# Six seams of a decoder layer, put in another order

## The chip, the cores and the metric

The program runs on one core of a Trainium2 chip. The metric is the device time of one execution in microseconds (us); lower is better. PE is the matrix engine (PEld its weight loads), DVE the vector engine, ACT the scalar engine, POOL the GpSimd engine, and SP the queue that issues DMAs here. Each engine works through its own instructions in the order in which the program lists them and waits for others by semaphores, so the order of the listing is the schedule.

## The reference, cut to what matters

```python
x = x + attn(layernorm(x))                  # 8 x 112 tokens, 512 wide, 16 heads of 32, rotary, causal
ln = layernorm(layernorm(x)) * ln_w + ln_b
q, k, v = lin(fp8(ln / q_in)), lin(fp8(ln / k_in)), lin(fp8(ln / v_in))    # 16 / 8 / 8 heads of 128
qx = lin(fp8(ln / qx_in)); kx, vx = ctx @ w_kv_x                           # ctx: 8 x 375 x 512
core, xout = gqa(norm(q), norm(k), v), gqa(norm(qx), norm(kx), vx)
x = x + fp8(concat(core, xout) / smooth) @ wproj * scale
h = silu(g) * u                              # (g, u) = layernorm(x) @ ternary(w_gate_up)
x = x + rms_norm(h) @ ternary(w_proj)        # hidden width 2048
```
`fp8` clips to 448 and rounds to a float8 and back. The result has 8 x 112 rows of 512 numbers.

## The kernel before

The whole layer is one straight program; nothing is looped on the chip. Its stages, with the lines of the listing:

The first attention takes the 8 batches in two halves of four. It loads x tiles `xb` (L94), `vec` (all small vectors, L99) and weights; DVE works out constants from `vec` (L117 to L145: inverse scales `rins`, `lnw`, `lnb`, `rsm`, `psc`, `epsc`, `hln`); `norm_stats` and `norm_apply` make the normed rows `h`, PE transposes them (L375), and `project_qk` (L388) makes queries and keys with the rotary turn on DVE and POOL. Per batch, `batch(b, last)` (L535) lists: `values(b)`, `attended(b-2)`, `scores(b)` (L438), `turned(b-1)` (transposes of the weights, L471, and their copy `pt`), and `softmaxed` (DVE adds the mask, L451, and reduces, L458; POOL subtracts, L459; ACT takes the exponential, L462). `joined` adds the output to `xb` and norms the sum again; `to_tiles` (L533) copies the sums by DMA from tiles of 112 rows to tiles `xs` of 128.

The rounding to float8 of the second norm's output is cut into 32 tiles: 2 halves x 4 column chunks k x 4 scale sets m (query, key, value, context query). `qgroups` lists groups that share one transposed input: PE transposes it once into a PSUM buffer (`quantise_turn`, L297), and `quantise_begin` (L304) lets ACT make `y` (scale and bias, L315) and `big` (L227). At a group's last tile it also has the next group transposed ahead. `quantise(n, begin)` (L318) lists n steps: a begin (if asked), for an earlier tile the two clips on DVE (L231, L232) and the sum `f8t` on POOL (L234), and for a still earlier one the subtraction into `xq[m]` on DVE (L333). Calls stand in the last two projections, in the batches, and after the first units. PSUM has four buffers `ps` and four `pa`, each handed out in turn.

Weights of the second attention come through `load_raw` from a queue; `split_chunk(s, what, k)` (L258) splits one chunk into a high and a low part on ACT and DVE or POOL and then lists the next load on SP. The second attention then runs as 64 units: 32 `Own` (4 sets s of heads x 8 batches b) and 32 `Context` units. A unit's `project` lists its projections and, between them, later stages of earlier units through `advance(stage, g)`:

```python
            advance("score", g)
            advance("turn_p", g)
            advance("out", g)
            self.pkv = pa()
```
`score` is q times k (L739); `weigh` takes exponentials (L753), the reciprocal `ri` (L638) and the product on POOL (L640); `turn_p` transposes it (L762); `out` is the output projection of five units earlier (`project_out`, L597 with `cq`). `own_background` lists weight splits at the end of each own unit. At unit 32 the pools of the own units close, and the first weights `wx` and context tile `ct` of the context units are loaded (`load_wx`, `load_ct`); `keys(j)` (L801) multiplies them.

The feed-forward makes `hid` in blocks of 256 with the sums of squares `sq` (POOL, L1067); `down(c, hid, last)` (L1177) projects down. In the last call it first sums `sq` over partitions by PE (L1182), takes the root on POOL, and then per tile of 128 rows adds the product to `ys`, scales by `rstd`, adds `xs` and stores.

Of the kernel before, what the change touches and what calls it, by code (L numbers as in the profile page):

```python
# [11 lines left out]
F32 = mybir.dt.float32  # L12
# [7 lines left out]
P = 128  # L20
# [18 lines left out]
def decoder_layer(  # L39
# [73 lines left out]
    nc.gpsimd.memset(gones[64:128, 64:128], 1.0 / 128.0)  # L113

    rins = const.tile([P, 16], F32, tag="rins", name="rins")  # L117
    nc.vector.reciprocal(rins, vec[:, V_INS : V_INS + 16])
    lnw = const.tile([P, 16], F32, tag="lnw", name="lnw")
    lnb = const.tile([P, 16], F32, tag="lnb", name="lnb")  # L120
    for m in range(4):
        cut = slice(4 * m, 4 * m + 4)
        nc.vector.tensor_mul(lnw[:, cut], rins[:, cut], vec[:, V_LNW : V_LNW + 4])
        nc.vector.tensor_mul(lnb[:, cut], rins[:, cut], vec[:, V_LNB : V_LNB + 4])
    rsm = const.tile([P, 32], F32, tag="rsm", name="rsm")
    nc.vector.reciprocal(rsm, vec[:, V_SM : V_SM + 32])
    nc.vector.tensor_scalar_mul(rsm[:, 0:16], rsm[:, 0:16], vec[:, V_SC + 2 : V_SC + 3])
    psc = const.tile([P, 1], F32, tag="psc", name="psc")
    nc.vector.tensor_mul(psc, vec[:, V_SC + 5 : V_SC + 6], vec[:, V_SC + 4 : V_SC + 5])

    epsc = const.tile([P, 4], F32, tag="epsc", name="epsc")
    nc.vector.tensor_mul(epsc, vec[:, V_SC : V_SC + 4], vec[:, V_SC : V_SC + 4])
    nc.vector.reciprocal(epsc, epsc)
    nc.vector.tensor_scalar_mul(epsc, epsc, LN_EPS)
    sgn = const.tile([P, 4], F32, tag="sgn", name="sgn")
    nc.vector.tensor_scalar(sgn, vec[:, V_SC : V_SC + 4], 0.0, 2.0, ALU.is_ge, ALU.mult)
    nc.vector.tensor_scalar_add(sgn, sgn, -1.0)

    hln = const.tile([P, 8], F32, tag="hln", name="hln")
    for i, (sg, f) in enumerate(((0, ISD), (None, ISD), (1, 1.0), (None, 1.0), (3, ISD), (None, ISD), (None, 1.0), (None, 1.0))):  # L140
        v = vec[:, V_HLN + i : V_HLN + i + 1]
        if sg is None:
            nc.vector.tensor_scalar_mul(hln[:, i : i + 1], v, f)
        else:
            nc.vector.tensor_scalar(hln[:, i : i + 1], v, sgn[:, sg : sg + 1], f, ALU.mult, ALU.mult)  # L145


    def col(i):
        return vec[:, i : i + 1]
# [154 lines left out]
    def quantise_begin(t):  # L304
        i, half, k, m = qtiles[t]
        if m == qgroups[i][2][0]:
            if ("tp", i) not in qstate:
                quantise_turn(i)
            qstate["ln"] = qstate.pop(("tp", i))[:, :SH]
        if m == qgroups[i][2][-1] and i + 1 < len(qgroups) and qgroups[i + 1][0] == half:  # L310
            quantise_turn(i + 1)
        y = s0.tile([P, SH], BF, tag="y", name=uid("y"), bufs=4)

        at = slice(4 * m + k, 4 * m + k + 1)
        nc.scalar.activation(y, qstate["ln"], AF.Identity, bias=lnb[:, at], scale=lnw[:, at])  # L315
        qstate["y", t] = round_begin(y, s0, 6)

    def quantise(n, begin=True):  # L318


        for _ in range(n):
            if begin:
                quantise_begin(qstate["begun"])
                qstate["begun"] += 1
# [12 lines left out]

    with ExitStack() as st:
# [166 lines left out]
        for b in range(HB):  # L505
            ln_apply(b)
        transposed(0)
        for i, oc in enumerate((0, 4, 1, 5, 2, 6, 3, 7)):
# [26 lines left out]
        def batch(b, last):  # L535

            least = last - HB
            if b < last:
                va[b] = values(b)
            if b - 2 >= least:  # L540
                attended(b - 2, va.pop(b - 2), pt.pop(b - 2))
            if b < last:
                banks = scores(b)
            if least <= b - 1 < last:
                pt[b - 1] = turned(pr.pop(b - 1))
            if b < last:
                pr[b] = softmaxed(banks)

# [2 lines left out]
        for i, oc in enumerate((0, 4, 1, 5, 2, 6, 3, 7)):  # L551
            project_qk(1, oc)
            if i < 2:
                batch(HB + i, HB)
            if i < HB + 2:
                joined(i, 0, HB)
            else:
                quantise(2)
        first.close()
        for b in range(HB, B):  # L560
            batch(b, B)
            quantise(3)
            if b >= HB + 2:
                joined(b - 2, HB, B)

# [9 lines left out]
        to_tiles(b)  # L575
    for b in range(B, B + 2):
        batch(b, B)
        quantise(2 + b - B, False)
        joined(b - 2, HB, B)
        for k in range(2):  # L580
            split_chunk(0, 0, 2 * (b - B) + k)
        to_tiles(b - 2)
    second.close()
    for b in range(B, B + 2):
# [84 lines left out]
    class Own(Unit):  # L669
# [5 lines left out]
        def project(self, g):  # L675
# [248 lines left out]

    def own_background(s, b):

        if b < 4:
            split_chunk(s, 2, b)
        if s < 3 and b in (4, 5):
            split_chunk(s + 1, 1, b - 4)  # L930
        if b >= 5:
            split_chunk(s + 1, 0, b - 5)
        if b == 7:
            split_chunk(s + 1, 0, 3)
            if s < 3:
                split_chunk(s + 1, 1, 2)
                split_chunk(s + 1, 1, 3)
# [237 lines left out]
    expand_w("down", 0)  # L1175
    ys = [f1.tile([P, H], F32, tag=f"y{t}", name=f"y{t}") for t in range(NT)]
    def down(c, hid, last):  # L1177
        wd = wfs.pop(("down", c))
        if last:
            pr = ps()  # L1180
            for t in range(NT):
                nc.tensor.matmul(  # L1182
                    pr[:, t : t + 1], lhsT=sq[:, t * P : (t + 1) * P], rhs=ones1, start=True, stop=True
                )
            rstd = sm("rms", NT)
            nc.vector.tensor_scalar(rstd, pr[:, 0:NT], 1.0 / FF, RMS_EPS, ALU.mult, ALU.add)
            power(rstd)
        for t in range(NT):
            po = ps()
            for k in range(4):  # L1190
# [7 lines left out]
                    )  # L1198
            if c == 0:
                nc.vector.tensor_copy(ys[t], po)  # L1200
            else:
                nc.vector.tensor_tensor(ys[t], ys[t], po, ALU.add)
            if last:
                nc.vector.scalar_tensor_tensor(
                    ys[t], ys[t], rstd[:, t : t + 1], xs[t], ALU.mult, ALU.add
                )
# [104 lines left out]
```

## Time and profile before

| | |
|---|---|
| median of 3 runs | 1376.29 us (1372.47 to 1377.64) |
| profiled execution | 1375.96 us |
| its span | 1373.9 us |
| mean granted clock of PE | 0.954 |
| busy: PE, DVE, ACT, POOL | 1267.4, 879.2, 737.8, 806.2 us |

The profile is of one execution. A group line names the source line, the engine, the operation, out<-in by tile names, the shapes and the count; then busy time and the mean of one; then the idle time of the engine just ahead, with what ended it. A timeline line begins with the start and the length in us; a bracket at its end is the wait ahead of it and what ended that. A stretch line gives the stretch, its length, the busy time of PE, PEld, DVE, ACT and POOL with counts, the granted clock of PE as a share of full, the busy share of the DMA engines, and GB/s.

### The profile page before, as it was taken

Reading aid. Unit: us, or ns where it says so; the run is one execution under the profiler, and the core shown is the slowest. Engines: PE = TensorE matmul, PEld = TensorE weight load, DVE = VectorE, ACT = ScalarE, POOL = GpSimd, SP = SyncE. Lnnn points to the kernel's source line nnn. Section 1 sums busy time; section 2 is a strip of 40 time slices with the busy share of each in tenths; the row PEclk is TensorE's granted clock in tenths of the full one; section 3 lists DMA queues with packets and bytes.
Section 4 is the critical chain, followed back from the end, with each engine's and each line's share of the span. In section 5 each row is a group of like instructions: output and inputs, shape, how many; then the busy total and the mean of one; then the engine's idle time right before and its main releaser. Section 6 shows DMA issues by size and latency. Waiting matters only on the chain.

```text
span 1373.9 us, 18218 instructions
## 1 busy us (share of the span) xinstructions
PE 1267.4 (92%) x5890; PEld 902.3 (66%) x5890; DVE 879.2 (64%) x2274; ACT 737.8 (54%) x1918; POOL 806.2 (59%) x894
## 2 busy tenths in 40 slices
PE   5997875799999979999999999999999999889998
PEld 3563654688887855666666666666666566678886
DVE  5657777767677733556777777777778754543334
ACT  1334556767677725565565555655556545443432
POOL 4657766667676724446676666765767664343332
PEclk9998756999999989999999999999999999999999
DMA  5001120011111031222223323133221211001001
GB/s 160 1 1 54 34 83 23 32 55 40 54 39 54 25 108 51 76 77 91 84 76 107 95 96 98 64 105 108 91 80 57 92 49 66 0 31 47 24 0 54
DMA packets 41103, 85.24 MB, mean 62 GB/s; under 512 B 4800, under 2 KB 11072, under 8 KB 41008
## 3 DMA queue, kind: packets, MB, share of 16 engines
q1 hardware_dynamic: 41008, 84.08, 19.2%
q8 instruction: 47, 0.77, 0.2%
q14 instruction: 48, 0.39, 0.1%
HBM read 74.10 MB, written 8.13 MB: 60 GB/s over the span
## 4 chain that ended last, share of the span: by engine, by line
PE 77%; POOL 8%; DVE 7%; ACT 5%; issue 2%; DMA 1%; SPq 0%; POOLq 0%; ACTq 0%; DVEq 0%
PE pa L801 24%; PE pa L597 8%; PE pa L1078 7%; PE ps L597 7%; PE ps L903 5%; PE ps L870 5%; PE ps L1192 4%; PE ps L891 3%; PE ps L487 2%; PE pa L388 2%; PE ps L627 1%; PE ps L855 1%; POOL p L640 1%; PE ps L770 1%; PE ps L415 1%
## 5 line engine op out<-in xcount | busy, mean ns | idle before, releaser
L801 PE MATMUL pa<-wx,ct 128*125 128x512 f32 x768 | 348.3, 596 | 5.9 <-DMA ct<-in_ctxT 4.6
L801 PEld LDWEIGHTS pa<-wx,ct 128*125 128x125 f32 x768 | 141.5, 189 | 150.3 <-issue 145.7
L197 DVE BATCH_NORM_STATS2 bst<-pa 128x6 f32<-128x128 f32 (+1 forms) x472 | 130.7, 277 | 151.9 <-PE pa L801 114.9
L234 POOL TENSOR_TENSOR f8t<-y,big 128x512 f32<-128x512 bf16 (+1 forms) x88 | 103.4, 1181 | 207.1 <-DVE big L232 207.1
L640 POOL TENSOR_TENSOR p<-p,ri 112x448 f32<-112x448 f32 (+1 forms) x64 | 117.4, 1836 | 52.9 <-DVE ri L638 50.3
L879 ACT ACTIVATE p<-ps,cmx 112x375 f32<-112x375 f32 x128 | 71.8, 573 | 114.7 <-DVE cmx L878 114.7
L632 ACT ACTIVATE qT<-ps,hln 128x448 f32<-128x448 f32 (+6 forms) x112 | 57.3, 564 | 123.4 <-PE ps L627 123.3
L597 PE MATMUL pa<-hi,xq 128*128 128x512 f32 (+2 forms) x352 | 110.4, 339 | 12.4 <-DVE xq L333 9.0
L597 PE MATMUL pa<-lo,xq 128*128 128x512 f32 (+2 forms) x352 | 107.3, 331 | 5.3 <-DVE lo L275 5.3
L1078 PE MATMUL pa<-h3T,wf 128*128 128x512 f32 (+1 forms) x512 | 106.0, 367 | 0.0
L1078 PEld LDWEIGHTS pa<-h3T,wf 128*128 128x128 f32 x512 | 93.7, 190 | 10.4
L198 DVE BATCH_NORM_AGGREGATE mv<-bst 128x2 f32<-128x6 f32 (+1 forms) x472 | 86.0, 182 | 16.1
L597 PE MATMUL ps<-hi,cq 128*128 128x512 f32 x224 | 93.4, 417 | 1.3 <-POOL cq L660 1.1
L597 PE MATMUL ps<-lo,cq 128*128 128x512 f32 x224 | 90.4, 403 | 0.0
L870 PE MATMUL ps<-kT,qT 128*112 128x375 f32 x256 | 86.3, 479 | 0.8 <-DVE kT L860 0.7
L217 ACT ACTIVATE k<-pa,ckvnm,ckvr 125x128 f32<-125x128 f32 x192 | 79.9, 483 | 10.2 <-POOL ckvnm L213 10.2
L1067 POOL TENSOR_TENSOR sq<-sq,s 128x512 f32<-128x512 f32 (+1 forms) x30 | 34.6, 1154 | 81.8 <-ACT s L1066 81.8
L903 PEld LDWEIGHTS ps<-pT,v 125*128 125x128 f32 x384 | 73.1, 191 | 14.1 <-issue 13.9
L597 PEld LDWEIGHTS pa<-hi,xq 128*128 128x128 f32 (+1 forms) x352 | 67.4, 192 | 20.1 <-DVE xq L333 10.5
L903 PE MATMUL ps<-pT,v 125*128 125x224 f32 x384 | 78.4, 354 | 0.0
L217 ACT ACTIVATE q<-pa,cqnm,cqr 128x128 f32<-128x128 f32 x112 | 42.2, 458 | 65.1 <-POOL cqnm L213 65.1
L597 PEld LDWEIGHTS pa<-lo,xq 128*128 128x128 f32 (+1 forms) x352 | 67.2, 191 | 13.7 <-DVE lo L275 9.1
(158 smaller groups left out, 2952.4 us busy)
## 6 DMA issues: line engine op xcount, KB each, us to landing
ct<-in_ctxT SPq DMA_DIRECT2D x32, 750.0 KB, 4.4
w<-in_wattn SPq DMA_DIRECT2D x80, 256.0 KB, 3.0
tr<-in_wgu SPq DMA_DIRECT2D x32, 256.0 KB, 4.4
done<-th SPq DMA_DIRECT2D x48, 128.0 KB, 4.4
wh<-done SPq DMA_DIRECT2D x24, 256.0 KB, 2.9
wx<-in_wattn SPq DMA_DIRECT2D x16, 256.0 KB, 5.3
tr<-in_wdown SPq DMA_DIRECT2D x16, 256.0 KB, 4.5
w<-in_wqkv SPq DMA_DIRECT2D x12, 256.0 KB, 6.5
```

Of the source, the lines that this page charges most:

```text
L197: nc.vector.bn_stats(st[: self.rows], a)
L198: nc.vector.bn_aggr(self.mv[: self.rows, self.at, :], st[: self.rows])
L217: nc.scalar.activation(dst, src, AF.Identity, bias=self.nm[:rows, i : i + 1], scale=self.r[:rows, i : i + 1])
L234: nc.gpsimd.tensor_tensor(t, y16, big, ALU.add)
L597: nc.tensor.matmul(out_, lhsT=lhsT, rhs=part[:, cut], start=first and i == 0, stop=last and i == 1)
L632: nc.scalar.activation(qTs[u.s, b][:, :, rows], tp3[:, :, cut], AF.Identity, bias=hcol(ln + 1), scale=hcol(ln))
L640: nc.gpsimd.tensor_tensor(u.p, u.p, bc, ALU.mult)
L801: nc.tensor.matmul(pkv[:CJ, :], lhsT=ct[:, k, j * CJ : (j + 1) * CJ], rhs=wx[self.s, k], start=(k == 0), stop=(k == KC - 1),)
L870: nc.tensor.matmul(pp[:S, :SC], lhsT=qT[:, j, :], rhs=self.kT[:, j // 2, :], start=True, stop=True,)
L879: nc.scalar.activation(self.p[:, j, :], pp[:S, :SC], AF.Exp, bias=nm[:S], accum_out=self.sums[:S, j : j + 1])
L903: nc.tensor.matmul(po[:, cut], lhsT=self.v[:, j, g * P : (g + 1) * P], rhs=self.pT[:, j, cut], start=(j == 0), stop=(j == NJ - 1),)
L1078: nc.tensor.matmul(pp[:, :n], lhsT=wcur[k][:, m * 256 + blk * P : m * 256 + (blk + 1) * P], rhs=hT[half, k][i], start=(k == 0 and i == 0), ...
```

## The change

Six places are listed in another order. The arithmetic is the same but for the last scaling, where `ys*r + xs` and `po*r` are now two scaled sums.

1. First norms and constants: the constants move behind the first norms and transposes of half 0; 36 transposes of the identity are listed on PE at the start.
2. Begin of rounding: `quantise_begin` has no transpose ahead any more. In a batch four begins stand between `turned` and `softmaxed`.
3. Groups of rounding: the first half is begun in blocks of four and ends one batch earlier; in the own units the last four tiles are begun one per unit (units 3 to 6) and ended in units 7 and 8; the four splits of set 0's output weights move from units 0 to 3 to units 3 (two), 4 and 5.
4. Output projection: `out` is listed ahead of `turn_p` in an own unit.
5. First context tile: `load_ct` ahead of `load_wx`; the splits that closed the last own unit come after the cast `xqx` of the first context unit.
6. Last sums of squares: in the last `down` they stand behind the second tile's product.

```diff
+    idle = ps()
+    for _ in range(36):
+        nc.tensor.transpose(idle[:, :P], ident, ident)
...
-        if m == qgroups[i][2][-1] and i + 1 < len(qgroups) and qgroups[i + 1][0] == half:
-            quantise_turn(i + 1)
...
         for b in range(HB):
             ln_apply(b)
         transposed(0)
+        rins = const.tile([P, 16], F32, tag="rins", name="rins")
...
                 pt[b - 1] = turned(pr.pop(b - 1))
+            for _ in range(begin):
+                quantise_begin()
             if b < last:
                 pr[b] = softmaxed(banks)
...
-            else:
-                quantise(2)
+            if i == HB + 2:
+                for _ in range(4):
+                    quantise_begin()
+            elif i == HB + 3:
+                quantise(4, False)
...
-            batch(b, B)
-            quantise(3)
+            batch(b, B, 4 if b < B - 1 else 0)
+            quantise(4, False)
...
-        quantise(2 + b - B, False)
         joined(b - 2, HB, B)
-        for k in range(2):
-            split_chunk(0, 0, 2 * (b - B) + k)
+        if b == B:
+            for k in range(KC):
+                split_chunk(0, 0, k)
...
+            advance("out", g)
             advance("turn_p", g)
-            advance("out", g)
...
-            own_background(self.s, self.b)
+            if self.i < 4 * B - 1:
+                own_background(self.s, self.b)
...
-        if b < 4:
+        if s > 0 and b < 4:
             split_chunk(s, 2, b)
+        elif s == 0 and b == 3:
+            split_chunk(s, 2, 0)
+            split_chunk(s, 2, 1)
+        elif s == 0 and b in (4, 5):
+            split_chunk(s, 2, b - 2)
...
+            load_ct(u.i)
             load_wx(4)
-            load_ct(u.i)
             expand_q(u.i)
+            own_background(3, B - 1)
...
-        elif u.i == B:
+        elif u.i == B + 2:
             gap.close()
...
-        if u.i < 5:
-            quantise((4, 5, 3, 2, 2)[u.i])
-        if u.i in (2, 5):
-            quantise(5, False)
+        if u.i < 7:
+            quantise((4, 5, 3, 1, 1, 1, 1)[u.i])
+        if u.i in (2, 7, 8):
+            quantise(5 if u.i == 2 else 3, False)
...
-            if last:
-                nc.vector.scalar_tensor_tensor(
-                    ys[t], ys[t], rstd[:, t : t + 1], xs[t], ALU.mult, ALU.add
-                )
-                nc.sync.dma_start(out=out[t * P : (t + 1) * P, :], in_=ys[t])
+                pos.append(po)
+            if last and t == 1:
+                pr = ps()
...
+            while last and t > 0 and pos:
+                i = t + 1 - len(pos)
+                r = rstd[:, i : i + 1]
+                nc.vector.scalar_tensor_tensor(ys[i], ys[i], r, xs[i], ALU.mult, ALU.add)
+                nc.vector.scalar_tensor_tensor(ys[i], pos.pop(0), r, ys[i], ALU.mult, ALU.add)
+                nc.sync.dma_start(out=out[i * P : (i + 1) * P, :], in_=ys[i])
```

More of the change, by code (lines that the diff above doesn't have):

```diff
@@ L113, in decoder_layer @@
     nc.gpsimd.memset(gones[64:128, 64:128], 1.0 / 128.0)
[L117 to L143, printed above, removed]
-        else:
-            nc.vector.tensor_scalar(hln[:, i : i + 1], v, sgn[:, sg : sg + 1], f, ALU.mult, ALU.mult)
+    idle = ps()
+    for _ in range(36):
+        nc.tensor.transpose(idle[:, :P], ident, ident)
     def col(i):
@@ L302, in quantise_turn, with quantise_begin @@
         qstate["tp", i] = tp
-    def quantise_begin(t):
+    def quantise_begin():
+        t = qstate["begun"]
+        qstate["begun"] += 1
         i, half, k, m = qtiles[t]
@@ L322, in quantise @@
             if begin:
-                quantise_begin(qstate["begun"])
-                qstate["begun"] += 1
+                quantise_begin()
             t = qstate["clipped"]
@@ L507, in decoder_layer @@
         transposed(0)
+        rins = const.tile([P, 16], F32, tag="rins", name="rins")
+        nc.vector.reciprocal(rins, vec[:, V_INS : V_INS + 16])
+        lnw = const.tile([P, 16], F32, tag="lnw", name="lnw")
+        lnb = const.tile([P, 16], F32, tag="lnb", name="lnb")
+        for m in range(4):
+            cut = slice(4 * m, 4 * m + 4)
+            nc.vector.tensor_mul(lnw[:, cut], rins[:, cut], vec[:, V_LNW : V_LNW + 4])
+            nc.vector.tensor_mul(lnb[:, cut], rins[:, cut], vec[:, V_LNB : V_LNB + 4])
+        rsm = const.tile([P, 32], F32, tag="rsm", name="rsm")
+        nc.vector.reciprocal(rsm, vec[:, V_SM : V_SM + 32])
+        nc.vector.tensor_scalar_mul(rsm[:, 0:16], rsm[:, 0:16], vec[:, V_SC + 2 : V_SC + 3])
+        psc = const.tile([P, 1], F32, tag="psc", name="psc")
+        nc.vector.tensor_mul(psc, vec[:, V_SC + 5 : V_SC + 6], vec[:, V_SC + 4 : V_SC + 5])
+        epsc = const.tile([P, 4], F32, tag="epsc", name="epsc")
+        nc.vector.tensor_mul(epsc, vec[:, V_SC : V_SC + 4], vec[:, V_SC : V_SC + 4])
+        nc.vector.reciprocal(epsc, epsc)
+        nc.vector.tensor_scalar_mul(epsc, epsc, LN_EPS)
+        sgn = const.tile([P, 4], F32, tag="sgn", name="sgn")
+        nc.vector.tensor_scalar(sgn, vec[:, V_SC : V_SC + 4], 0.0, 2.0, ALU.is_ge, ALU.mult)
+        nc.vector.tensor_scalar_add(sgn, sgn, -1.0)
+        hln = const.tile([P, 8], F32, tag="hln", name="hln")
+        for i, (sg, f) in enumerate(((0, ISD), (None, ISD), (1, 1.0), (None, 1.0), (3, ISD), (None, ISD), (None, 1.0), (None, 1.0))):
+            v = vec[:, V_HLN + i : V_HLN + i + 1]
+            if sg is None:
+                nc.vector.tensor_scalar_mul(hln[:, i : i + 1], v, f)
+            else:
+                nc.vector.tensor_scalar(hln[:, i : i + 1], v, sgn[:, sg : sg + 1], f, ALU.mult, ALU.mult)
         for i, oc in enumerate((0, 4, 1, 5, 2, 6, 3, 7)):
@@ L533, in to_tiles, with batch @@
                 nc.sync.dma_start(out=xs[t][rows, :], in_=xb[b][cut, :])
-        def batch(b, last):
+        def batch(b, last, begin=0):
             least = last - HB
@@ L556, in decoder_layer @@
                 joined(i, 0, HB)
-            else:
-                quantise(2)
+            if i == HB + 2:
+                for _ in range(4):
+                    quantise_begin()
+            elif i == HB + 3:
+                quantise(4, False)
         first.close()
         for b in range(HB, B):
-            batch(b, B)
-            quantise(3)
+            batch(b, B, 4 if b < B - 1 else 0)
+            quantise(4, False)
             if b >= HB + 2:
@@ L1177, in down @@
     def down(c, hid, last):
-        wd = wfs.pop(("down", c))
-        if last:
[L1180 to L1183, printed above, removed]
-                )
-            rstd = sm("rms", NT)
-            nc.vector.tensor_scalar(rstd, pr[:, 0:NT], 1.0 / FF, RMS_EPS, ALU.mult, ALU.add)
-            power(rstd)
+        wd, pos = wfs.pop(("down", c)), []
         for t in range(NT):
@@ L1200, in down @@
                 nc.vector.tensor_copy(ys[t], po)
-            else:
-                nc.vector.tensor_tensor(ys[t], ys[t], po, ALU.add)
-            if last:
-                nc.vector.scalar_tensor_tensor(
-                    ys[t], ys[t], rstd[:, t : t + 1], xs[t], ALU.mult, ALU.add
-                )
-                nc.sync.dma_start(out=out[t * P : (t + 1) * P, :], in_=ys[t])
+            elif not last:
+                nc.vector.tensor_tensor(ys[t], ys[t], po, ALU.add)
+            else:
+                pos.append(po)
+            if last and t == 1:
+                pr = ps()
+                for i in range(NT):
+                    nc.tensor.matmul(
+                        pr[:, i : i + 1], lhsT=sq[:, i * P : (i + 1) * P], rhs=ones1, start=True, stop=True
+                    )
+                rstd = sm("rms", NT)
+                nc.vector.tensor_scalar(rstd, pr[:, 0:NT], 1.0 / FF, RMS_EPS, ALU.mult, ALU.add)
+                power(rstd)
+            while last and t > 0 and pos:
[4 more added lines that the diff above has]
+                nc.sync.dma_start(out=out[i * P : (i + 1) * P, :], in_=ys[i])
     for u in range(NU):
```

## The prediction

> **What bounds the kernel now.** I read the busy table and the 40 slices first, then the chain of waits in order of time, then busy time by stretch, and last the timeline of each seam, engine by engine.
>
> ```profile
> PE 1267.4 (92%) x5890; PEld 902.3 (66%) x5890; DVE 879.2 (64%) x2274; ACT 737.8 (54%) x1918; POOL 806.2 (59%) x894
> PE   5997875799999979999999999999999999889998
> PEclk9998756999999989999999999999999999999999
> ```
> PE has work 92% of the time. The lost 8% and the low clock lie in the first seven slices, in slices 13 and 14 (about 480 to 505 us), and at the end. By stretch (PE, PEld, DVE, ACT, POOL busy, then granted clock):
>
> ```profile
> 119.70:195.20 75.50, 55.85 (x376) 41.43 (x373) 56.65 (x120) 36.86 (x67) 55.44 (x50) 0.70 0.21 63
> 195.20:240.00 44.80, 29.44 (x141) 23.57 (x142) 32.64 (x98) 31.27 (x76) 28.34 (x32) 0.67 0.13 42
> 240.00:290.00 50.00, 40.52 (x247) 34.35 (x246) 35.48 (x110) 36.72 (x108) 30.12 (x38) 0.90 0.16 48
> 290.00:478.00 188.00, 176.31 (x1126) 155.15 (x1124) 138.00 (x451) 138.07 (x439) 129.61 (x175) 0.99 0.14 42
> 478.00:506.00 28.00, 19.01 (x66) 13.07 (x67) 8.76 (x23) 10.22 (x29) 7.60 (x10) 0.76 0.36 121
> ```
> In the first three no engine is full: they are chains of waits, and PE's busy time is at a low clock besides. From 510 to 1180 us PE is busy 99% and the change touches nothing there.
>
> **First norms (gain 9 us).** Timeline of the start:
>
> ```profile
> 7.07 0.25 DVE L118 RECIPROCAL rins<-vec 128x16 f32<-128x16 f32 x1 [7.07 <-DMA vec<-in_vecs]
> 10.09 0.69 DVE L173 BATCH_NORM_STATS2 bst<-xb 112x6 f32<-112x512 f32 x1
> 13.87 3.25 PE L375 MATMUL ps<-ident,h 112*128 112x112 f32 x16 [13.87 <-DVE h L185]
> 17.18 13.61 PE L388 MATMUL pa<-hT,w 128*128 128x448 f32 x32
> ```
> DVE stands until `vec` lands, then makes constants for 3.0 us (7.07 to 10.09), then the norms. The four x tiles, issued before `vec`, landed at about 3.4, 4.0, 6.2 and 6.8 us (issue plus time to landing). With the constants behind the norms, the fourth statistic ends at 6.8+0.8 = 7.6 instead of 13.4; POOL's root (0.25+0.57) and the last `h` follow, so transposes end near 10.5 and the first projection starts at 11.1 instead of 17.18: 6.1 us. Its four weights land by 11.2 us, so they do not hold it. The moved constants (3.0 us) then sit on DVE between 9.4 and 12.4, where it idled until 22.5 before; first use of them is at 114 us. The 36 added transposes: 16 cold ones took 3.25 us, so 36 take at most 7.3 to 8.4, from 1.3 us (when `ident` is ready) to 9.7 at the latest against the first `h` at 8.3: they cost 0 to 1.4. They buy a warm start: the first 16 projection records took 7.61 us against 16 x 0.375 = 6.0, so 1.6 us. Then x tiles 4 to 7 (landed 16.3 to 19.0, unchanged) still arrive before DVE asks, and the 2.2 us that PE waited for `h` at 31 to 35 us shrink by about 1.3. Sum 9 (bounds 4 and 10: the low end has only the 3.0 of constants and 1).
>
> [...]
>
> **Groups and begin of rounding, first half (gain 10 us).** PE's waits in 119.7 to 195.2 us (total, times, longest), and two lines of POOL's timeline, the third and fourth subtraction of a batch:
>
> ```profile
> PE ps L471 <- ACT y L315: 4.5, 1, 4.5
> PE ps L471 <- DVE v L424: 4.4, 1, 4.4
> PE ps L487 <- ACT y L315: 3.1, 1, 3.1
> ```
> ```profile
> 151.85 0.93 POOL L459 TENSOR_TENSOR p<-p,amx 112x448 f32<-112x448 f32 x1 [0.25 <-DVE amx L458]
> 153.04 2.80 POOL L459 TENSOR_TENSOR p<-p,amx 112x448 f32<-112x448 f32 x1 [0.25 <-DVE amx L458]
> ```
> The transposes for the next group hold one of four PSUM buffers until four `y` are read out, and ACT reaches those `y` only behind the exponentials. Now all four begins (4 x 1.22 = 4.9 us of ACT) stand ahead of the exponentials, while DVE masks and reduces (4.7 us), and no buffer is held across a batch: these 12 us of waits go. What is late next is DVE: per batch softmax 4.7, four clips 1.5, four `xq` 0.6 to 1.5 each with a wait for POOL, `v` and `o` 1.9, some 13 us. Walking the queues, the softmax of batch 4 starts 2.8 us later than before (clips and two `xq` now ahead of `v`), that of batch 7 still 2.6 later (166.0 against 163.3). But then nothing of the first half is left to round: `o` of batch 7 comes at 179, its sum on POOL at 180.3, the copy of xb7 is issued at 180.5 instead of 190.94 (SP had stood behind two weight loads there; now they go before), and the key splits that wait for that copy start at 184.1 instead of 194.62. 10 us; bounds 0 (each later start kept) and 15 (no POOL stretch).
>
> **Second half of the rounding (gain 4 + 6 us).** Units 0 to 2 lose three output-weight splits (3 x 1.28 POOL, 3 x 0.6 ACT) from the POOL chain that PE waits for at 222 to 233 us (9.0 us on `xq`): 4 (0 to 7). In 240 to 290 us 9.5 us of PE idle and some 3 of low clock come from the flush of five tiles in unit 5, where DVE stood from 262.3 to 267.5 in four `xq`; its tiles are now spread, with the flush in units 7 and 8, and only the context phase needs them. The splits reappear in units 3 to 5 (5.1 us of POOL, which has 20 of 50 free). I take half: 6 (0 to 9).
>
> **Output projection (gain 5 us).** In 290 to 478 us PE waits 6.2 us for POOL's `p` before `turn_p` (7.9 to unit 31, less its 1.7). The projection (8 records, 1.86 us) now covers that; its input is a unit old. Queued behind the later transposes are ACT's `pT` and exponentials, about 1 us later, but `ri` stood behind statistics until 461.3 while the exponentials ended at 459.4, so 1 us fits. 5 (0 to 7).
>
> **First context tile (gain 11 us).**
>
> ```profile
> 490.39 1.84 SPq L1104 DMA_DIRECT2D wx<-in_wattn  x4
> 492.28 0.91 SPq L1098 DMA_DIRECT2D ct<-in_ctxT  x2
> 499.88 5.99 PE L801 MATMUL pa<-wx,ct 128*125 128x512 f32 x8 [4.63 <-DMA ct<-in_ctxT]
> ```
> SP stood behind two weight loads that waited for `lo`, then issued weights, then two context tiles at once: landing took 7.5 us. Now the tile goes first, right after unit 31's last matmul; at about 483 it is issued and at 487.5 landed (4.4 us, the median of such loads), weights by 490. The two splits move behind the cast `xqx`, which saves 1.3 on ACT and gives 0.5 to 0.8 back as PE waits for the last `lo`. Waits for `p` (1.7), the cast and the tile (4.6) and the low clock (about 1.2, 2.3 and 2.5) go: keys end at 494.5 instead of 505.9. 11; bounds 6 (tile as slow as before) and 12.
>
> **Last sums (gain 2 us).** PE waited from 1350.8 to 1354.94 for sums of squares; now the down projection starts at once and warm (12.8 us, as in earlier blocks), with the 14 sums (1.9) behind its second tile. DVE becomes the end: root at 1358.6, then 14 x 0.73 = 10.2, so 1368.9 instead of 1370.8. 2 (0 to 4).
>
> Sum 9+10+4+6+5+11+2 = 47. The profiled execution took 1375.96 us (span 1373.9 and 2.06 around it), 0.3 below the median 1376.29. Forecast 1375.96-47 = 1329.0.
>
> **Rivals.** *POOL and DVE lock each other (20%).* `p` goes from 0.93 to 2.80 us, and `xq` from 0.61 to 2.43, where they meet. A fourth tile in a batch costs another wait (1.81) and slow `xq` (1.51), 3.3 us; three such batches use up the 10, and the same meetings in units 0 to 8 the 4+6: 1329.0+20 = 1349.0. For it: the walk above has DVE late in every batch. Against: the tiles are the same number, and in units 0 to 2 POOL has less to do. [...]
>
> *The output projection closes a loop (3%, slower).* If `p`, `turn_p`, `pT`, exponentials and `ri` were the cycle of a unit, moving `turn_p` back would lengthen each of 23 units by 1.86 us (42.8), lose the 5 and unit 31's 3, and at a clock of 0.83, as in 340 to 350 us, add 176.31/0.83-176.31/0.99 = 34.3: 1329.0+85.1 = 1414.1. It decides where the exponentials end after the statistics; by 459.4 against 461.3 they don't.
>
> *The start does not do what it says (5%).* If x lands with `vec` only, 4 instead of 9: 1334.0. Inside the range.
>
> **Numbers.** Forecast case 72%, lock 20%, start 5%, loop 3%. Half of the unknown bounds together reach down to 1310; upward the lock case with a weak start gives 1354. Range 1310 to 1354. A difference under 0.5% (6.9 us) can't be told from none here. Slower: the loop, 3%. Same: lock in all seams at their low ends, 3%. Faster 94%.
>
> **What would show it.** First `bst` near 3.5 us and first projection near 11; no wait of L471 on `y`; key splits 19 us earlier than before on the clock of the span (10 and the 9 of the start); `turn_p` without waits; keys' first record about 46 us earlier; tail bound by DVE. Wrong if DVE's idle time before `xq` grows, or if PE's idle in 290 to 478 us exceeds its 11.7 now.

## The result, and the profile after

The changed kernel takes 1332.46 us (median of 4 runs, 1329.04 to 1334.62) against 1376.74 us before on the same chip: ratio 0.9682, 95% interval 0.9653 to 0.9711. The forecast was 1329.0 us, range 1310 to 1354. The span of the profiled execution fell from 1373.9 to 1331.0 us, by 42.9 where the sum said 47. That the total came so close is partly luck: two terms were far too large and one far too small.

The busy table and two of the slice lines of the changed kernel:

```profile
PE 1262.1 (95%) x5926; PEld 900.1 (68%) x5926; DVE 883.8 (66%) x2274; ACT 739.6 (56%) x1918; POOL 802.8 (60%) x894
PE   8997895899999999999999999999999999889998
PEclk9997866999999999999999999999999999899999
```

PE has the same work (5.3 us less busy time, 36 more records) in a shorter span. The border to the context units (480 to 505 us before) lay almost wholly in the fifteenth slice of the view before, not in 13 and 14 as the prediction counts; now it lies in slice 14, which is full. Ahead of the feed-forward only slices 4 to 8, and the first, stay low. Line numbers shift after the change: L388 is now L359, L597 is L607, L762 is L773, L801 is L812, L1192 is L1200.

The same marks read off both timelines show where the lead grew:

| mark | before | after | lead |
|---|---|---|---|
| first projection of the first attention | 17.18 | 10.23 | 6.95 |
| values of batch 4 | 119.73 | 112.14 | 7.6 |
| first key projection of unit 0 | 195.18 | 182.88 | 12.3 |
| ninth score of the own units | 301.76 | 281.50 | 20.3 |
| 30th score of the own units | 478.04 | 447.66 | 30.4 |
| first keys (`wx`, `ct`) | 499.88 | 459.72 | 40.2 |
| first context score | 533.42 | 490.87 | 42.6 |
| second context score | 558.37 | 517.48 | 40.9 |
| last context score | 1187.13 | 1147.67 | 39.5 |
| end of span | 1373.9 | 1331.0 | 42.9 |

The 30th score is the last one ahead of the context units; unit 31 lists it, and it is unit 29's own, since a score is listed two units later. The expectation of experiment 6 calls it the score of unit 31.

Busy time between these marks (stretch, its length, busy PE, PEld, DVE, ACT, POOL, granted clock, DMA share, GB/s), first before, then after:

```profile
119.73:195.18 75.45, 55.80 (x374) 41.38 (x372) 56.63 (x120) 36.81 (x67) 55.44 (x50) 0.70 0.21 63
195.18:301.76 106.58, 81.05 (x453) 67.70 (x453) 75.07 (x235) 75.65 (x207) 67.22 (x84) 0.81 0.14 43
301.76:478.04 176.28, 165.23 (x1060) 145.42 (x1058) 131.10 (x423) 130.46 (x415) 120.89 (x163) 0.99 0.15 43
478.04:499.88 21.84, 12.89 (x54) 10.31 (x55) 8.63 (x22) 10.18 (x29) 7.56 (x10) 0.79 0.43 144
```
```profile
112.14:182.88 70.74, 58.70 (x377) 43.53 (x376) 60.09 (x120) 35.05 (x63) 51.46 (x50) 0.76 0.23 68
182.88:281.50 98.62, 77.42 (x452) 65.96 (x453) 76.55 (x235) 75.66 (x207) 67.25 (x82) 0.86 0.15 46
281.50:447.66 166.16, 160.84 (x1059) 142.57 (x1058) 131.03 (x423) 131.84 (x415) 121.19 (x164) 1.00 0.16 45
447.66:459.72 12.06, 10.21 (x55) 7.87 (x56) 7.66 (x21) 8.68 (x25) 5.83 (x6) 1.00 0.57 195
```

Counts of work differ by at most four records in each pair of lines. In the first pair DVE's share rises from 75% to 85%, more than any other engine's there; experiments 2 and 3 ask whether it is the bound. In the third, PE's idle time falls from 11.05 to 5.32 us, but its busy time falls too, by 4.4 us, with no work removed; experiment 5 shows where.

The timeline of the start (PE, then DVE) and of the end of the changed kernel:

```profile
1.35 6.23 PE L118 MATMUL ps<-ident 128*128 128x128 f32 x36 [1.35 <-POOL ident masks.py:199]
7.76 2.13 PE L346 MATMUL ps<-ident,h 112*128 112x112 f32 x16 [0.19 <-DVE h L157]
10.23 12.29 PE L359 MATMUL pa<-hT,w 128*128 128x448 f32 x32 [0.34 <-ACT hT L352]
...
3.58 0.69 DVE L145 BATCH_NORM_STATS2 bst<-xb 112x6 f32<-112x512 f32 x1 [3.58 <-DMA xb<-in_x]
...
1310.28 3.79 PE L1200 MATMUL ps<-wf,hid 128*128 128x512 f32 x16
1313.90 1.62 PE L1216 MATMUL ps<-ones,sq 128*128 128x1 f32 x14
1315.38 9.37 PE L1200 MATMUL ps<-wf,hid 128*128 128x512 f32 x40
...
1327.16 0.75 DVE L1226 SCALAR_TENSOR_TENSOR y<-ps,rms,y 128x512 f32<-128x512 f32 x1
```

The first statistic is at 3.58 us, the 16 transposes of `h` take 2.13 us where they took 3.25 with no work of PE ahead of them. At the end the down projection runs on without a stop, and the last line is one of 14 on DVE with no wait between them, as forecast.

### The profile page after: what moved, and what is told of

Its sections match the earlier page's. It is cut to its first block, busy times and chain, and to the rows that moved or that the text cites. A ratio compares the mean times of both kernels' runs of the same rounds, so it can differ in the third digit from the quotient of the medians.

```text
span 1331.0 us, 18281 instructions
## 1 busy us (share of the span) xinstructions
PE 1262.1 (95%) x5926; PEld 900.1 (68%) x5926; DVE 883.8 (66%) x2274; ACT 739.6 (56%) x1918; POOL 802.8 (60%) x894
## 4 chain that ended last, share of the span: by engine, by line
PE 75%; DVE 11%; ACT 6%; POOL 6%; issue 2%; DMA 0%; POOLq 0%; SPq 0%; ACTq 0%; DVEq 0%
PE pa L812 24%; PE pa L607 8%; PE pa L1094 7%; PE ps L607 6%; PE ps L914 6%; PE ps L881 5%; PE ps L902 3%; PE ps L1200 3%; PE pa L359 2%; PE ps L637 2%; PE ps L781 2%; PE ps L866 1%; DVE xq L304 1%; DVE y L203 1%; PE ps L458 1%
## 5 line engine op out<-in xcount | busy, mean ns | idle before, releaser
L812 PE MATMUL pa<-wx,ct 128*125 128x512 f32 x768 | 346.8, 594 | 1.3 <-ACT v L858 1.3
L812 PEld LDWEIGHTS pa<-wx,ct 128*125 128x125 f32 x768 | 141.1, 188 | 144.6 <-issue 139.8
L607 PE MATMUL pa<-hi,xq 128*128 128x512 f32 (+2 forms) x352 | 112.2, 345 | 11.3 <-DVE xq L304 9.2
L607 PE MATMUL pa<-lo,xq 128*128 128x512 f32 (+2 forms) x352 | 106.9, 330 | 1.0 <-DVE lo L247 0.9
L607 PE MATMUL ps<-hi,cq 128*128 128x512 f32 x224 | 90.2, 403 | 2.2 <-POOL cq L670 1.1
L607 PE MATMUL ps<-lo,cq 128*128 128x512 f32 x224 | 87.9, 392 | 0.0
L189 ACT ACTIVATE k<-pa,ckvnm,ckvr 125x128 f32<-125x128 f32 x192 | 80.0, 483 | 10.1 <-POOL ckvnm L185 10.1
L914 PEld LDWEIGHTS ps<-pT,v 125*128 125x128 f32 x384 | 74.2, 194 | 14.4 <-issue 13.9
L607 PEld LDWEIGHTS pa<-hi,xq 128*128 128x128 f32 (+1 forms) x352 | 67.6, 192 | 18.0 <-DVE xq L304 10.7
L881 PEld LDWEIGHTS ps<-kT,qT 128*112 128x112 f32 x256 | 44.9, 176 | 42.8 <-issue 14.8
```

Source lines behind the costliest of these rows:

```text
L189: nc.scalar.activation(dst, src, AF.Identity, bias=self.nm[:rows, i : i + 1], scale=self.r[:rows, i : i + 1])
L607: nc.tensor.matmul(out_, lhsT=lhsT, rhs=part[:, cut], start=first and i == 0, stop=last and i == 1)
L812: nc.tensor.matmul(pkv[:CJ, :], lhsT=ct[:, k, j * CJ : (j + 1) * CJ], rhs=wx[self.s, k], start=(k == 0), stop=(k == KC - 1),)
L881: nc.tensor.matmul(pp[:S, :SC], lhsT=qT[:, j, :], rhs=self.kT[:, j // 2, :], start=True, stop=True,)
L914: nc.tensor.matmul(po[:, cut], lhsT=self.v[:, j, g * P : (g + 1) * P], rhs=self.pT[:, j, cut], start=(j == 0), stop=(j == NJ - 1),)
```

## The experiments

Each kernel below, but for the last two, is the changed kernel with one place put back or edited. One measurement of a kernel scatters by 2 to 8 us, about as much as one of these places is worth, so the verdicts rest on the length of the stretch in which the edit lies, and the times stand beside them. Stretches that are the same in several listings show how far that can be trusted: from batch 4's values to the first key projection eight of nine took 70.69 to 70.74 us and one, that of experiment 8, 71.09; from there to the ninth score nine took 97.7 to 98.6, from the ninth to the 30th score twelve took 165.6 to 166.2. Ahead of batch 4 the scatter is wider: its values started anywhere from 110.8 to 115.1 us where the start was that of the changed kernel.

**1. First half of the rounding as before.**

```diff
-            batch(b, B, 4 if b < B - 1 else 0)
-            quantise(4, False)
+            batch(b, B)
+            quantise(3)
...
+        quantise(2 + b - B, False)
         joined(b - 2, HB, B)
-        if b == B:
-            for k in range(KC):
-                split_chunk(0, 0, k)
+        for k in range(2):
+            split_chunk(0, 0, 2 * (b - B) + k)
```
(the transposes ahead in `quantise_begin` are back too, for these 16 tiles, and so is `quantise(2)` in the last two projections)

> The changed kernel, but the first half of the rounding is listed as before (transposes ahead, two or three tiles a call, flush and key splits behind the last batches); the second half, the start, the output projection and the rest stay changed. The prediction's own term: 10 us lost, so about 1342.5 against 1332.5. By the marks of the changed trace (lead over before 7.6 us at the values of batch 4, 12.3 us at the first key projection) 4.7 us: about 1337, first key projection at 187.6 instead of 182.9, waits of the weights' transposes on y of about 7 us back. Rival, that the stretched operations of DVE and POOL ate the whole gain: 1332.5, key projection within 1 us of 182.9.

Measured: 1336.49 us, ratio 0.9722 (0.969 to 0.9754); span 1332.7. From batch 4's values to the first key projection 75.51 us against 70.74, and 75.45 before: this place is worth 4.8 us, not 10 and not 0. PE's waits in 112 to 188 us, with the old listing and then with the new:

```profile
PE ps L444 <- ACT y L289: 4.4, 1, 4.4
PE pa L606 <- DVE lo L247: 4.4, 1, 4.4
PE ps L444 <- DVE v L397: 4.4, 1, 4.4
PE ps L460 <- ACT y L289: 3.1, 1, 3.1
```
```profile
PE ps L442 <- DVE v L395: 3.8, 2, 3.2
PE pa L409 <- DVE p L422: 3.5, 4, 1.4
PE ps L442 <- ACT pt L446: 2.8, 4, 1.3
```

The two waits on `y` (7.5 us) go, as forecast, and so does a wait of 4.4 on a weight split. The third of the prediction's 12 us, on DVE's `v`, does not: 4.4 become 3.8 (L444 there is L442 here). With it, 10.1 us of waits are left in the new listing, 7.3 of them on DVE, where the old one had 5.1 on the same three tiles.

**2. The same 16 sums on DVE instead of POOL.** In `round_a` the addition of tiles 0 to 15 is `nc.vector.tensor_tensor`.

> The changed kernel with the sums f8t of the first 16 tiles on DVE instead of POOL; nothing left out. If the clips of 0.27 us take 1.1 to 1.2 only because POOL is at work beside them (six of eight before batch 4, so about 5 us, and per batch one clip and one xq by 0.9 each and a wait of 1.8), then the softmax of batch 4 starts 2 us earlier, each batch takes 12.3 instead of 13.7, and the key projection comes 4 to 6 us earlier: 1327 to 1329. Rival, DVE is simply full: 16 more sums of 0.54 come on top and the time grows by up to 8.6 us to 1341.

Measured: 1331.27 us, 0.9675 (0.9653 to 0.9697); the stretch 71.48 us, 0.7 longer. Neither expectation held as put. The stretching does come from POOL's work beside DVE: of the eight clips ahead of batch 4's softmax five take 1.1 to 1.2 us in the changed kernel, and one with the sums on DVE. First the changed kernel, then the sums on DVE:

```profile
115.62 1.20 DVE L203 TENSOR_SCALAR y<-y 128x448 bf16<-128x448 bf16 x1
```
```profile
118.50 0.27 DVE L203 TENSOR_SCALAR y<-y 128x448 bf16<-128x448 bf16 x1
...
127.20 1.01 POOL L432 TENSOR_TENSOR p<-p,amx 112x448 f32<-112x448 f32 x1 [0.25 <-DVE amx L431]
```

The same clip takes 0.27 us or 1.1 to 1.2, and the fourth subtraction 1.01 instead of 2.83. But the time saved so is filled by the sums themselves: DVE was busy 60.81 of the 64.96 us from 112.14 to 177.10, against 56.06.

**3. Less work for DVE in the batches.**

```diff
-                nm = sm("amx", 4)
-                nc.vector.tensor_reduce(nm[:S], p, AX.X, ALU.max, negate=True)
-                nc.gpsimd.tensor_tensor(
-                    p, p, nm[:S].rearrange("p (h o) -> p h o", o=1).to_broadcast([S, 4, S]), ALU.add
-                )
```

> The changed kernel; left out is the subtraction of the largest score ahead of the exponential in the first attention: the reduction amx on DVE (4 x 0.54 = 2.2 us a batch) and the subtraction on POOL (5.6 us a batch, 2.80 of it beside DVE's clips). If the batches are bound by DVE, the batch of 13.7 us falls by at least the 2.2, and by 1.8 to 3.5 more where DVE waited for POOL, 4 to 5.7 in all: over four batches the first key projection comes 10 to 16 us earlier than 182.9, and the time is 1317 to 1323. If they are bound by PE at its low clock (66% busy there) or by ACT (begins, exponentials and copies, 9.3 us a batch), less than 5 us: over 1328.

Measured: 1318.91 us, 0.9591 (0.9574 to 0.9607); span 1316.6. The stretch falls from 70.74 to 57.79 us, 12.95, inside the 10 to 16 of the first theory; the softmax of one batch starts 9.0, 11.3 and 10.9 us behind that of the one before instead of 12.6, 13.7 and 13.7. From batch 4's values to the first query projection:

```profile
111.19:161.86 50.67, 44.44 (x366) 32.18 (x364) 45.35 (x92) 33.45 (x62) 29.42 (x29) 0.90 0.22 66
```

DVE is still at 90%, and PE was granted 0.90 of its clock. Experiment 2 had halved POOL's work in the batches (24.57 for 48.42 us in 112.14 to 177.10) and gained nothing, while DVE took the work over; here, with 8.9 us of reductions off DVE and POOL's subtraction no longer beside it, the stretch falls by 13 us, where its whole reordering was worth 4.8. Both point to DVE as the bound of the batches. The edit also takes the hand-over to POOL out of every softmax, and how much of the 13 us is due to that was not separated.

**4. Second half of the rounding as before.** `quantise((4, 5, 3, 2, 2)[u.i])` for units 0 to 4, flushes in units 2 and 5, and `if b < 4: split_chunk(s, 2, b)` for all sets.

> The changed kernel with the second half of the rounding as before: begins 4, 5, 3, 2, 2 in units 0 to 4, five tiles flushed in unit 5, output-weight splits in units 0 to 3. The prediction's two terms: 4+6 = 10 us lost, 1342.5. By the marks (lead from 12.3 at the first key projection to 20.3 at the score at 281.5, less what the output projection gives in three units) 7 us: about 1339.5. Rival, that those units are bound by something else (the first waits on xq stay at 9 us in both): 1332.5.

Measured: 1336.70 us, 0.9709 (0.9684 to 0.9734); span 1335.3. From the first key projection to the ninth score 103.99 against 98.62 us: 5.4. By intervals between scores it is 2.4 us between the first two, -0.1 in the next three, 6.4 in the two around the flush in unit 5, and -3.3 later, since the changed kernel pays for its own flush there (11.48 against 8.16 us). PE's longest waits in that stretch:

```profile
PE pa L607 <- DVE xq L304: 10.5, 2, 7.3
PE ps L637 <- ACT q L189: 5.7, 1, 5.7
PE ps L737 <- DVE x L625: 4.6, 1, 4.6
```

In the changed kernel the first two are 9.2 and 4.5 us, so moving the splits is worth 2.5 us here; but before, with all else old, they were 9.0 and 4.6. The wait on `x` is the one that the spread of the flush removes.

**5. The transposes of the weights ahead of the output projection.** `advance("turn_p", g)` and `advance("out", g)` change places.

> The changed kernel with the transposes of the weights listed ahead of the output projection again, as before. The prediction's term: 5 us lost, 1337.5. By the marks (lead over before grows from 20.3 to 30.4 us between the scores at 281.5 and 447.7): 10 us, of which 5.7 idle and 4.4 in longer matmuls, so about 1342.6. Rival, that the growth comes from the spread of the rounding and not from this place: 1332.5.

Measured: 1348.64 us, 0.9795 (0.977 to 0.982); span 1346.6. This is the dearest place of the six: 18.2 us from the first key projection to the first keys (5.8 to the ninth score, 9.8 to the 30th, 2.7 in the border to the context units), where the prediction said 5 and the marks 10. Waits on POOL's `p` from the ninth to the 30th score, first in this kernel, then in the changed one:

```profile
PE ps L773 <- POOL p L650: 6.8, 9, 1.7
```
```profile
PE ps L773 <- POOL p L650: 0.7, 2, 0.4
```

The waits differ by 6.1 us, the stretch by 9.8. An ordinary unit takes 8.44 us instead of 8.19 though its idle time is only 0.03 to 0.05: its transposes begin when `score` has ended (304.56 behind 304.52), where in the changed kernel the projection begins 0.23 us ahead of that end (298.57 against 298.80). So the block covers the end of `score` besides the wait. The two borders between sets in this stretch take 12.38 and 10.66 instead of 9.51 and 9.54, with 1.4 and 1.1 us more idle and, at the first, a clock of 0.86, which is 1.7 us of its 12.38. The 5.8 us in the first units depend on the other place: put back alone, the rounding costs 5.4 and this order 5.8; both put back (the kernel before) cost 8.0, so either alone gains 2.2 or 2.6, and 3.2 of the gain comes only with both.

**6. Weights ahead of the first context tile, splits ahead of the cast.**

```diff
-            load_ct(u.i)
             load_wx(4)
+            load_ct(u.i)
             expand_q(u.i)
-            own_background(3, B - 1)
```

> The changed kernel with the weights ahead of the first context tile and the last splits ahead of the cast, as before. The prediction's term: 11 us lost, 1343.5. By the marks (lead 30.4 at the score of unit 31, 42.6 behind the first keys): 12.2 us, 1344.7, less up to 3 that the changed kernel loses in the context units, where the same waits of 2.0 and 2.5 us were followed by a lower clock: 1341.7 to 1344.7. Rival, that the tile was not what the keys waited for: the wait is then on the weights, and the time within 3 us of 1332.5.

Measured: 1340.22 us, 0.975 (0.9736 to 0.9765); span 1338.4. From the 30th own score to the first keys 19.51 us against 12.06, and from there to the first context score 32.89 against 31.15: 9.2 in all. PE's longest wait from 447 to 480 us:

```profile
PE pa L811 <- DMA ct<-in_ctxT: 5.0, 1, 5.0
```

The next is 2.6 us on the cast `xqx`. In the changed kernel there is no wait on the tile and 1.4 us on the cast. The tile, issued as one of two behind the weights, is what the keys wait for; alone and first it is not.

**7. Sums of squares ahead of the last down projection.** The old ending of `down`, with the sums under `if last:` ahead of the loop.

> The changed kernel with the sums of squares ahead of the last down projection and the old three-step ending, as before. The prediction's term: 2 us lost, 1334.5; by the marks (23.1 us from the last hidden matmul to the end before, 20.6 after) 2.5: 1335. Rival, that the saving is the warm clock alone and DVE bounds both: 1332.5.

Measured: 1336.35 us, 0.9716 (0.9694 to 0.9738); span 1330.9, since this execution was 1.3 us ahead at batch 4 and lost less in the context units. From the last hidden matmul to the end of the span, the stretch in which the edit lies, it takes 23.1 us, as before, against 20.6: 2.5. Of the twelve executions of the new ending eleven took 20.6 and one 21.8. From the first hidden matmul the difference is 3.4 (177.80 against 174.38), but 0.9 of that lies in the hidden blocks, which the edit does not touch and which took 153.8 to 155.2 us over all executions.

**8. Constants ahead of the first norms, the 36 transposes kept.**

> The changed kernel with the constants on DVE ahead of the first norms again; the 36 transposes stay. The first statistic goes back from 3.6 to about 10 us and the first projection from 10.2 to about 16.5, for DVE stood for the small vectors. If the clock stays up over the 5 to 6 us between the last added transpose (7.6) and the first transposes of h (13.4), the loss is about 6 us: 1338.5. If it falls again (the first 16 projections take 7.6 us as before instead of about 6), about 8 us: 1340.5. Rival, that the start was bound by the landing of x and not by the constants: 1332.5.

Measured: 1339.34 us, 0.9745 (0.9726 to 0.9764); span 1333.5. The first projection starts at 17.80 us, 7.6 later; at batch 4's values 5.0 of that are left (2.0 to 6.3 against the starts of the other executions). The start of PE:

```profile
14.49 3.25 PE L378 MATMUL ps<-ident,h 112*128 112x112 f32 x16 [6.60 <-DVE h L189]
```

After 6.60 us without work the 16 transposes take 3.25 us again, at a granted clock of 0.50, and the 36 added ones, done at 7.9 us, bought them nothing.

**9. No added transposes.**

> The changed kernel without the 36 added transposes. If they buy a warm clock: first transposes of h 3.25 instead of 2.13 us and the 32 first projections 13.6 instead of 12.3, 2.4 us in all, still there at the values of batch 4 (114.5 instead of 112.1): 1335. Rival, that the second x tiles or DVE take the gain back before the first batch: 112.1 there, 1332.5.

Measured: 1333.39 us, 0.9701 (0.9683 to 0.9719); span 1330.8. The transposes of `h` take 3.25 us instead of 2.13 and the first 32 projections 13.01 instead of 12.29, though the granted clock reads 1.00 there in both kernels; the second half's transposes are 1.5 us later. At batch 4's values nothing is left (112.14 in both). That is uncertain by the scatter ahead of batch 4, so the added transposes are worth between nothing and 1.5 us.

**10. Sums of the own units' tiles on DVE.** As in 2, for tiles 16 to 31.

> The changed kernel with the sums f8t of tiles 16 to 31 (those of the own units) on DVE instead of POOL; nothing left out. There DVE is not full (46 of 62 us in 183 to 245), and PE waits 9.2 us for xq and 4.5 for q. If a tile's path is what PE waits for (clips, of which one in two is stretched to 1.1, sum 1.28 and hand-overs: 1.75 us a tile), it falls to about 1.45 and the waits of 13.7 by 3 to 5 us: 1327 to 1329. If DVE's longer queue delays the statistics instead, as the first half showed, no gain: 1331 to 1335.

Measured: 1330.19 us, 0.967 (0.9654 to 0.9685), beside 1332.13 for the changed kernel in the same comparison, so no difference by the time; by the marks 95.38 us instead of 98.62 from the first key projection to the ninth score. The wait on `q` falls from 4.5 to 2.8 us, that on `xq` only from 9.2 to 9.0.

**11. The changed kernel again.**

> The changed kernel itself once more. Two places far behind the change take 24.95 or 26.6 us (from the first to the second context score) and 12.4, 13.9 or 15.4 us (between the last two) in the eight profiles so far, with the same waits of 2.0 and 2.5 us in them. If that is a state of the clock that comes anew in each execution, this profile shows other values than 26.61 and 15.33, or its span other than 1331.0 by such a step; if it belongs to the listing, the same values within 0.1.

Measured: 1332.13 us, 0.9686 (0.9671 to 0.97); span 1331.7. Two stretches of the same listing came out otherwise: batch 4's values at 114.08 instead of 112.14, and 13.93 instead of 15.33 us between the last two context scores. These are the rows of the last two scores in the changed kernel, in this repetition and in the kernel of 8:

```profile
1132.34:1147.67 15.33, 12.08 (x47) 9.60 (x46) 5.97 (x16) 7.46 (x21) 6.16 (x8) 0.78 0.00 1
```
```profile
1133.47:1147.40 13.93, 10.67 (x48) 8.45 (x46) 5.96 (x16) 7.47 (x21) 6.15 (x8) 0.88 0.01 1
```
```profile
1136.72:1149.11 12.39, 9.15 (x48) 6.71 (x46) 5.96 (x16) 7.26 (x21) 6.14 (x8) 1.00 0.01 1
```

The work and the wait in it (2.5 us, on `p`) are the same; the clock granted behind the wait is 0.78, 0.88 or 1.00.

**12. Both edits that paid, 3 and 10.**

> The changed kernel with both edits that paid: no subtraction of the largest score in the first attention (left out, as in e9_no_max) and the sums f8t of tiles 16 to 31 on DVE. They lie in different stretches, so they should add: 13 us from the batches (70.7 to 57.8 between the values of batch 4 and the first key projection) and 3.2 us from the own units (98.6 to 95.4 up to the score of unit 8): 1332.1-16 = 1316. If the units are bound by something that only the earlier start brings up (the landing of their weights), the second part is missing: 1319.

Measured: 1319.28 us, 0.9599 (0.9583 to 0.9614); span 1315.8. It does not beat experiment 3: from the first key projection to the ninth score 98.20 us against 98.05. The first interval is 1.8 us shorter, as in 10, but the second is 0.7 longer and the one that ends at the ninth score, at a clock of 0.86 in place of 1.00, 0.8 longer. Of the 3.2 us of experiment 10, which are 2.3 against the shortest of the nine stretches above, nothing is left here. The fastest kernel is that of experiment 3; the softmax is the same when any number is taken from all scores of a row, but without that step large scores would overflow.

## Why the prediction was right, step by step

| step | forecast | lead by the marks | by putting it back |
|---|---|---|---|
| first norms, constants, added transposes | 9 | 7.6 | 5.0 (2.0 to 6.3); the transposes alone 0 to 1.5 |
| rounding, first half | 10 | 4.7 | 4.8 |
| rounding, second half | 4+6 | 8.0, with the output projection | 5.4 |
| output projection | 5 | 10.1 from the ninth score on | 18.2 in all |
| first context tile | 11 | 12.2 | 9.2 |
| last sums | 2 | 3.4, of which 0.9 ahead of the edit | 2.5 |
| context units | 0 | -3.1 | |
| sum | 47 | 42.9 | |

The last column need not add up: the two places in the own units count 3.2 us of shared gain twice.

*Right in mechanism and size:* the first statistic (3.58 against 3.5), the first projection (10.23 against 11.1), the tile (11 against 9.2 to 12.2: issued right behind unit 31's last matmul, and no wait for it is left), the last sums (2 against 2.5). The wait for `h` that was to shrink by 1.3 us did not (1.05 and 1.20 are still there), and the 1.6 us counted for a warm start show in the first transposes and projections (1.1 and 0.7 us) but not surely at batch 4. Two signs came smaller with the terms behind them: the key splits start 12.3 us earlier (182.32 for 194.62), not 19, and behind `h` now, no longer behind the copy of the sum; the first keys come 40.2 us earlier, not 46.

*First half of the rounding, mis-sized: 10, measured 4.8.* No wait on `y` is left and DVE is next, as the prediction said. Its walk of the queues was short. It let batch 4's softmax start 2.8 us later than before and counted the four clips of a batch at 1.5 us; on before's clock it started 5.1 later (121.89+7.6 against 124.43). Of the eight clips ahead of it five take 1.1 to 1.2 us instead of 0.27, beside POOL's last rotary products and four sums: 4.4 us. The softmax of batch 7 then came at 169.5 on that clock, not 166.0, and its `o` at 185.6, not 179, for the last `attended` ran 6.05 us at a clock of 0.50 (at 154 us, at 1.00, one took 3.24). So up to batch 7's softmax the new order lost 6.2 us, not the 2.6 of the walk, and from there to the key projection it gained 10.9 (20.94 for 31.85), not 12.6. A part of the lock rival happened, in the start of the rounding above all; experiment 2 shows that moving the sums to DVE instead gains nothing, and experiments 2 and 3 point to DVE as the bound.

*Second half, mis-sized: 10, measured 5.4.* The 4 us for the splits taken off POOL were too much: 2.5 by putting them back, and against before the two waits did not get shorter (13.7 us for 13.6). Experiment 10 shows that the engine of the sum hardly moves the one on `xq`; what it hangs on was not settled. The 6 us for the flush were right in place (6.4 there), but 3.3 of it come back in units 7 and 8, which the prediction did not price.

*Output projection, mis-sized: 5, measured 10 in its stretch and up to 18.* Only the idle time in 290 to 478 us was counted. The 4.4 us of PE's busy time that fell besides are the clock at one border between sets (0.83 in 340 to 350 us before, 1.7 us; the like in experiment 5) and, for the most part, the ends of `score` that nothing covered. The first units and the last border gain too (5.8 and 2.7).

*The rivals.* The long rows that the lock rival starts from came again (the clip 0.27 or 1.1 to 1.2 us, `p` 0.93 or 2.83) and cost some of the first half, 4.4 us ahead of batch 4's softmax, not the 20 us of its case. The loop did not close: `ri` and `pT` follow without trouble, PE's wait on `pT` rose from 1.6 us in 195 to 302 us to 3.1, and the place is the largest gain of all. That the start does less than it says (5%) was nearer to what happened, 5.0 to 7.6. Of the two signs named as fatal, neither came: DVE's idle time ahead of `xq` fell from 14.6 to 9.5 us, and PE's idle time in the last own units fell.

*What no step had:* 3.1 us lost in the context units, whose code and waits the change does not touch.

## What to carry to other kernels

When a reordering removes waits on one engine, add up the work of the next one over the whole stretch, with the durations that its rows have when the other engine runs beside it (here 1.1 to 1.2 us for a clip of 0.27), not the short ones; that sum, and not the waits removed, says what is left to gain. A short wait of the matrix engine cost more here than its idle time: the independent block of matmuls listed ahead of it was worth 9.8 us from the ninth to the 30th score, where the wait table says 6.1. Before reading a few us as the effect of an edit, profile the same kernel twice and read only the stretches that come out the same.

## What the runs showed of the hardware that was not expected

The granted clock behind the same wait differs between executions. Over 14 profiles (before, after, twelve experiments) the stretch between the first two context scores, with one wait of 2.0 us, took 24.94 to 24.95 us five times and 26.60 to 26.63 nine times; that between the last two, with one of 2.5, took 12.4 us twice, 13.9 seven times and 15.3 to 15.6 five times. The changed kernel itself gave 15.33 and 13.93: the clock was 0.50 for 6.8 us in the one (1138.88 to 1145.70) and for 3.4 in the other (1140.60 to 1144.01). Between the first two scores its two profiles agree (26.61 and 26.63), so there a change without an edit is not shown. The mean clock between them was 1.00 before (24.95 us) and 0.94 in the changed kernel. So behind waits of 2.0 and 2.5 us the clock fell to 0.50 in some executions and stayed at 1.00 in others; what decides between the two was not shown. The 3.1 us that the changed kernel lost in the context units are such steps, 1.7 and 1.4.

Being busy did not bring the clock back at once: from 165 to 178 us of the changed kernel PE was busy 12.61 of 13.00 us, with transposes and with matmuls 33 columns wide, at a granted clock of 0.50.

One operation's length differs by a factor of up to four with what the other engine runs beside it. The 128x448 clip in bf16 on DVE took 0.27 us, and 1.1 to 1.2 beside POOL's products and sums; POOL's subtraction took 0.93 us, and 2.83 beside DVE's clips, which stayed at 0.27 there; DVE's `xq` took 0.61 us, and up to 2.42. Which of the two engines is the one held up, and why, was not shown.
